# A click predictor's early groups: the recurrence's state as the stationary operand of the first layer

## The chip, the cores and the metric

The kernel runs on one core of one Trainium2 chip. The metric is the device time of one execution in microseconds (us); lower is better. The core has TensorE (PE: matrix products from SBUF into PSUM, each with a weight load of its stationary operand, PEld), VectorE (DVE), ScalarE (ACT), GpSimd (POOL) and SyncE (SP), each with an instruction queue of its own that runs in order. Data come and go by DMA, which SP, POOL and ACT issue.

## The reference

For 1024 users (B) with a history of 100 items (T) of 128 features, all in fp32:

```python
_, gru_seq = scan(gru_step, h0, swapaxes(item_historical_embedding, 0, 1))
keys = swapaxes(gru_seq, 0, 1)
feat = concatenate([keys, q, keys - q, q * keys], axis=-1)      # q: the item, for each step
score = mlp(feat, 80 -> 40 -> 1, relu);  score = where(mask == 1, score, -inf)
attn = softmax(score, axis=1)
pooled = einsum('bt,btd->bd', attn, keys);  att_seq = pooled.T[:T]

def augru_step(h, (x_t, a_t)):                   # second recurrence, over the keys
    r = sigmoid([h, x_t] @ Wr.T + br);  u = a_t[:, None] * sigmoid([h, x_t] @ Wu.T + bu)
    h_hat = tanh([h * r, x_t] @ Wh.T + bh)
    return (1 - u) * h + u * h_hat
attention_feature = the state of step sequential_length - 1 of each user
comb = concatenate([user, item, hist_sum, item * hist_sum, attention_feature], axis=1)   # 640
scores = mlp(comb, 640 -> 200 -> 80 -> 1, sigmoid)               # the predictor; one number a user
```

A user's second recurrence is needed only up to the user's own length.

## The kernel before

Activations lie with features on the 128 partitions and users along the free axis, so a layer is a matmul whose stationary operand is a block of weights. The users are two halves (`NH` = 2) of `HB` = 512.

The first phase (`gru_phase`, up to about 1400 us) runs the first recurrence, the attention network, the softmax and the pooled sums, and computes for each user the part of the predictor's first layer that needs no recurrence, 200 sums per user (`features`), stored as rows in `part_d`. It also ranks the users by length. The change doesn't touch it.

The second phase (`augru_phase`) runs the second recurrence with the users sorted by falling length and dealt to the two halves in turn, so that a step t works on the first `widths[t]` users of each half alone: 512 at t = 0, 428 at t = 18, 70 at t = 88, 32 at the end. There are three copies of the phase, for three sets of widths, of which a count of the lengths chooses one; the data here take the set named `WIDTHS[0]`. The order on every queue is the order in which the program issues (a manual schedule).

`half_step(t, i)` issues, for one half: on TensorE the closing matmul of the other half's candidate (`ph<-r`, line 1131), then this half's `pr` and `pu` from the state `h_all`, then the three opening matmuls of the next half-step from the keys (line 1127); on ScalarE a tanh (line 1139) and two sigmoids (1151, 1152); on VectorE the product with tanh (1155), `r` (1157), the other half's new state `h_all` (1159), `pu` times the attention (1165), `rest` (1168) and then a transpose of keys for two steps ahead (1117). TensorE needs `r` for the next half-step's first matmul and `h_all` for its second. From `one` on (t = 88, 70 users or fewer in a half) `whole_step(t)` takes both halves at once.

Gathers of the keys' rows (`load_row`, lines 187 and 188) run on GpSimd's queue, each behind a one-column copy of `rest`, which paces them.

`predict(g)` is the predictor for a group of 64 users of each half (`PR` = 64, 128 users together). It is a generator: each `yield` is a stop, and the main loop advances the oldest job by one stop per half-step (in whole steps twice per step), from the ninth half-step after the group's last user has ended. Groups 7 to 1 so end within the recurrence, at steps from t = 18 (group 7) to t = 93 (group 1); group 0 (`last`) runs behind the recurrence. In order, a job gathers its rows of `part_d` into `part` (128 users x 200, line 1279); forms the first layer's sums `p0` (two chunks of `MC` = 100 features x 128 users) by transposing `part` onto PSUM with a matmul against the identity (`of_part`, line 1286) and adding the state's product (`of_state`, line 1291: weights stationary, 64 columns of the state moving, once per half); applies the sigmoid (1326); and goes through the second layer (1332, 1337), the third (1340, 1343) and a scatter of the 128 results to `early_d` (line 1345, issued on GpSimd's queue by `rows_of`, line 1271). At the end `earlier_results` loads all early results into `all_y` (line 1381), and the last group adds its own by four matmuls `po` (1349) and a VectorE sum (1357) ahead of the store.

Early jobs take their PSUM tiles from `pa`, a pool of one bank: a job's next tile waits until the last one is read.

Of the kernel before, what the change touches and what calls it, by code (L numbers as in the profile page):

```python
# [9 lines left out]
F32 = mybir.dt.float32  # L10
# [9 lines left out]
P = 128  # L20
B = 1024
T = 100
HB = 512
NH = B // HB
# [7 lines left out]
M0, M1 = 200, 80  # L32
MC = 100
# [44 lines left out]
PR = P // NH  # L78
# [5 lines left out]
def kernel(ctx: ExitStack, tc: tile.TileContext, a: dict, out: bass.AP):  # L84
# [26 lines left out]
    nc = tc.nc  # L111
# [24 lines left out]
    ident = const.tile([P, P], F32, name="ident")  # L136
# [6 lines left out]
    h_all = const.tile([P, NH, HB], F32, name="h_all")  # L143
    h3 = [h_all[:, i, :] for i in range(NH)]
# [15 lines left out]
    rows = {}  # L160
# [828 lines left out]
    def augru_phase(pools, widths, alive):  # L989
# [6 lines left out]
        sp = pools.enter_context(tc.tile_pool(name="sp3", bufs=2))  # L996
# [3 lines left out]
        one = min((t for t in range(T) if widths[t] <= ONE), default=T)  # L1000
# [12 lines left out]
        def bank(name, n=None):  # L1013

            if n is None:
                n = ring.pop(0)
                ring.append(n)
            return ps[n].tile([P, HB], F32, tag="g", name=name)
# [240 lines left out]
        def predict(g, last=False):  # L1259


            m0, m1 = later["m0"], later["m1"]
            n = M0 // MC
            tag = "last" if last else "a"

            def of_pool(name):
                return bank(name) if last else pa.tile([P, HB], F32, tag="a", name=name)


            def rows_of(out_ap, in_ap, o, i):  # L1270
                nc.gpsimd.indirect_dma_start(
                    out=out_ap,
                    out_offset=o and bass.IndirectOffsetOnAxis(ap=idx_p[:, g : g + 1], axis=0),
                    in_=in_ap,
                    in_offset=i and bass.IndirectOffsetOnAxis(ap=idx_p[:, g : g + 1], axis=0),
                )

            part = sp.tile([P, M0], F32, tag=f"part_{tag}", name="part3")
            rows_of(part, part_d, None, True)
            yield  # L1280
            f0 = sp.tile([MC, n, P], F32, name="f0")
            p0 = [of_pool("p0") for _ in range(n if last else 1)]
            p0 = [p0[j if last else 0][:MC, ts(0 if last else j, P)] for j in range(n)]

            def of_part(j):
                nc.tensor.matmul(  # L1286
                    p0[j], lhsT=part[:, ts(j, MC)], rhs=ident, start=True, stop=False
                )

            def of_state(j, i):  # L1290
                nc.tensor.matmul(  # L1291
                    p0[j][:, ts(i, PR)],
                    lhsT=m0[:, 4, ts(j, MC)],
                    rhs=h3[i][:, ts(g, PR)],
                    start=False,
                    stop=i == NH - 1,
                )

            if last and one < T:
                for j in range(n):  # L1300
                    of_part(j)
                yield
                for j in range(n):
                    nc.tensor.matmul(
                        p0[j].rearrange("p (i r) -> p i r", i=NH),
                        lhsT=m0[:, 4, ts(j, MC)],
                        rhs=h_all[:, :, ts(g, PR)],
                        start=False,
                        stop=True,
                    )  # L1310
                yield
            elif last:
                for j in range(n):
                    of_part(j)
                for i in range(NH):
                    for j in range(n):
                        of_state(j, i)
                    yield
            else:
                for j in range(n):  # L1320
                    of_part(j)
                    for i in range(NH):
                        of_state(j, i)
                yield
            for j in range(n):
                nc.scalar.activation(
                    f0[:, j, :], p0[j], AF.Sigmoid, bias=later["c0"][:, j : j + 1]
                )
            yield
            p1 = of_pool("p1")[:M1, :P]  # L1330
            for j in range(n):
                nc.tensor.matmul(  # L1332
                    p1, lhsT=m1[:, j, :], rhs=f0[:, j, :], start=(j == 0), stop=(j == n - 1)
                )
            yield
            f1 = sp.tile([M1, P], F32, name="f1")
            nc.scalar.activation(f1, p1, AF.Sigmoid, bias=later["c1"])
            yield
            p2 = of_pool("p2")[:, 0:1]
            nc.tensor.matmul(p2, lhsT=f1, rhs=later["m2"], start=True, stop=True)  # L1340
            yield
            y = sp.tile([P, 1], F32, name="y")
            nc.scalar.activation(y, p2, AF.Sigmoid, bias=later["c2"])
            if not last:
                rows_of(early_d, y, True, None)
                return
            p = of_pool("po")[:, :BQ]
            for q in range(P // R):
                nc.tensor.matmul(
                    p[ts(q, R), :],  # L1350
                    lhsT=y.to_broadcast([P, R]),
                    rhs=later["places"][q // 2][:, ts(q % 2, BQ)],
                    start=True,
                    stop=True,
                )
            all_y = later["all_y"]
            nc.vector.tensor_add(all_y, p, all_y)
            nc.sync.dma_start(
                out=out.rearrange("(q c) -> q c", c=BQ),
                in_=all_y.rearrange("(q r) c -> q r c", r=R)[:, 0, :],  # L1360
            )
# [65 lines left out]
        for t in range(1, T):  # L1427
# [23 lines left out]
            for g in range(1, HB // PR):  # L1451
                if left <= g * PR < alive[t]:
                    jobs.append([0, predict(g)])
                    if left:
                        next(jobs[-1][1])
            if t == T - G:
                final = predict(0, last=True)
                next(final)
# [98 lines left out]
```

## Time and profile before

| | us |
|---|---|
| median of 3 timed runs | 2017.4 |
| lowest, highest | 2016.58, 2022.05 |
| the profiled execution | 2009.0 |
| its span, first to last instruction | 2007.1 |
| TensorE busy in the span | 1983.7 |
| VectorE busy | 1671.7 |
| GpSimd busy | 1274.2 |
| ScalarE busy | 934.8 |

The profile is one execution; times within it count from the start of its span. A row of a group or of the timeline names line, engine, operation, the tiles written and read, and the shape; in timeline rows of TensorE the shape is first the stationary operand (128*100: 128 rows, 100 columns), then the moving one, and "x2" joins two records that follow each other. An fp32 matmul leaves two records of about equal length. Matmuls overlap, so the sum of their durations is more than the time that they take; the distance between starts is the better measure. In a row of stretches, behind the stretch and its length, stand the busy us (and instructions) of PE, PEld, DVE, ACT and POOL, then the granted share of TensorE's clock, the DMA engines' share and GB/s.

### The profile page before, as it was taken

The numbers are of one execution on the slowest core, as the hardware profiler recorded it, in microseconds if no ns is written. First come the engines' busy times: TensorE is split into PE (matmuls) and PEld (weight loads), VectorE is DVE, ScalarE is ACT, GpSimd is POOL, SyncE is SP. The second block draws the span as 40 slices with busy tenths as digits, with TensorE's granted clock in tenths as the row PEclk, the third lists the DMA queues.
The fourth block names the chain that finished last, engine by engine and source line by source line (L and its number), as shares of the span: only waits on it lengthen the run. The fifth ranks groups of instructions, "written<-read, shape, count | busy, mean of one in ns | idle before, by whom it ended". The sixth has DMA issues, their size and how long they took to land. (4 is left out here: it accounts for less than half of the span.)

```text
span 2007.1 us, 41031 instructions
## 1 busy us (share of the span) xinstructions
PE 1983.7 (99%) x15380; PEld 994.6 (50%) x15380; DVE 1671.7 (83%) x3010; ACT 934.8 (47%) x1672; POOL 1274.2 (63%) x1325
## 2 busy tenths in 40 slices
PE   9999999999999999999999999998899999999998
PEld 2334444444444444444444444434444556678997
DVE  7878999887978888888878798998577777888985
ACT  4444454454544454544444454554343444444553
POOL 0233939669796959496896868898774353445331
PEclk9999999999999999999999999999999999999998
DMA  4443333333334434333333333333443343333331
GB/s 125 98 118 92 107 99 106 91 83 106 115 106 109 121 103 125 115 104 102 103 105 106 107 92 107 108 91 94 123 132 99 94 112 95 93 101 99 84 79 32
DMA packets 242075, 204.85 MB, mean 102 GB/s; under 512 B 59506, under 2 KB 204890, under 8 KB 241866
## 3 DMA queue, kind: packets, MB, share of 16 engines
q1 hardware_dynamic: 227514, 169.37, 30.2%
q0 software_dynamic: 12480, 32.04, 5.8%
q8 instruction: 123, 2.02, 0.4%
q10 hardware_dynamic: 1872, 0.72, 0.1%
q14 instruction: 86, 0.70, 0.1%
HBM read 146.01 MB, written 54.41 MB: 100 GB/s over the span
## 5 line engine op out<-in xcount | busy, mean ns | idle before, releaser
L534 PE MATMUL ps<-x,wih 128*32 128x512 f32 x4800 | 616.3, 593 | 0.0
L534 PE MATMUL ps<-hn,whh 128*32 128x512 f32 x4752 | 610.7, 592 | 1.4 <-ACT hn L582 1.4
L534 PEld LDWEIGHTS ps<-x,wih 128*32 128x32 f32 x4800 | 216.1, 110 | 302.0 <-issue 298.7
L534 PEld LDWEIGHTS ps<-hn,whh 128*32 128x32 f32 x4752 | 214.3, 110 | 298.9 <-issue 295.3
L519 POOL TENSOR_TENSOR xm<-x,m 128x512 f32<-128x512 f32 x200 | 234.9, 1174 | 143.2 <-DMA m<-mask_d 142.9
L546 ACT ACTIVATE r<-ps,brz 128x512 f32<-128x512 f32 x200 | 137.7, 689 | 386.3 <-PE ps L534 386.1
L520 POOL TENSOR_TENSOR hist<-hist,xm 128x512 f32<-128x512 f32 x200 | 257.9, 1290 | 15.7
L188 POOL DMA_INDIRECT rows<-keys_d,idx_k x218 | 211.5, 970 | 80.7 <-POOL rows L187 72.5
L637 POOL TENSOR_TENSOR pooled<-pooled,kw 128x512 f32<-128x512 f32 x191 | 245.0, 1283 | 15.0
L636 POOL TENSOR_TENSOR kw<-kt,e 128x512 f32<-128x512 f32 x191 | 206.2, 1080 | 69.7 <-DVE e L809 69.6
L565 ACT ACTIVATE ps<-ps,bih 128x512 f32<-128x512 f32 x200 | 132.4, 662 | 229.4 <-DVE ps L564 229.4
L700 PE MATMUL pm<-hn,wk 128*32 128x512 f32 x1200 | 221.8, 592 | 0.0
L700 PE MATMUL pm<-kq,wkq 128*32 128x512 f32 x1200 | 221.7, 592 | 0.0
L1139 ACT ACTIVATE c<-ph,bh 128x510 f32<-128x510 f32 (+57 forms) x174 | 88.3, 507 | 261.1 <-PE ph L1131 261.0
L554 DVE SCALAR_TENSOR_TENSOR u<-ps,bhh,r 128x512 f32<-128x512 f32 x198 | 147.5, 745 | 71.3 <-PE ps L534 68.6
L700 PE MATMUL pm<-mv,w 128*32 128x512 f32 (+1 forms) x808 | 195.4, 592 | 0.6 <-DVE e L790 0.6
L569 DVE TENSOR_TENSOR d<-hn,ps 128x512 f32<-128x512 f32 x198 | 136.1, 687 | 35.9 <-ACT ps L565 35.7
L564 DVE TENSOR_TENSOR ps<-ps,u 128x512 f32<-128x512 f32 x200 | 140.0, 700 | 25.9 <-remote 4.5
L582 ACT COPY hn<-ps 128x512 f32<-128x512 f32 x200 | 116.6, 583 | 93.5 <-DVE kq L576 91.8
L570 DVE TENSOR_TENSOR d<-ps,d 128x512 f32<-128x512 f32 x200 | 138.4, 692 | 26.0 <-ACT ps L566 11.6
L187 POOL COPY rows<-rest 128x1 f32<-128x1 f32 x202 | 38.4, 190 | 175.4 <-DVE rest L1168 170.0
L571 DVE TENSOR_TENSOR ps<-ps,d 128x512 f32<-128x512 f32 x200 | 139.9, 700 | 6.8
(224 smaller groups left out, 3111.8 us busy)
## 6 DMA issues: line engine op xcount, KB each, us to landing
x<-in_hist_x SPq DMA_DIRECT2D x210, 256.0 KB
keys_d<-kt SPq DMA_DIRECT2D x48, 1024.0 KB
m<-mask_d SPq DMA_DIRECT2D x200, 128.0 KB
rows<-keys_d,idx_k POOLq DMA_INDIRECT x218, 3.0
s_b<-mv SPq DMA_DIRECT2D x200, 8.0 KB
keys_d<-kt SPq DMA_DIRECT2D x32, 64.0 KB
mask_i<-in_mask SPq DMA_DIRECT2D x8, 200.0 KB
part_d<-part SPq DMA_DIRECT2D x2, 400.0 KB
```

The costliest lines, as they stand in the source:

```text
L188: nc.gpsimd.indirect_dma_start(out=r[:, at, :], out_offset=None, in_=keys_d[q], in_offset=bass.IndirectOffsetOnAxis(ap=idx_k[:, k, i : i + ...
L519: nc.gpsimd.tensor_mul(d, x, m)
L520: nc.gpsimd.tensor_add(acc, acc, d)
L534: nc.tensor.matmul(p[ts(q, R), :], lhsT=w[:, g, ts(q, R)], rhs=v, start=(j == 0), stop=(j == len(parts) - 1),)
L546: nc.scalar.activation(r, pr, AF.Sigmoid, bias=brz[:, 0:1])
L554: nc.vector.scalar_tensor_tensor(out=u, in0=ph, scalar=bhh[:, 2:3], in1=r, op0=ALU.add, op1=ALU.mult,)
L564: nc.vector.tensor_add(pi, pi, u)
L570: nc.vector.tensor_mul(d, pz, d)
L571: nc.vector.tensor_add(pi, pi, d)
L636: eng.tensor_mul(d, k, w)
L637: eng.tensor_add(acc, acc, d)
L700: nc.tensor.matmul(p[i][s, :], lhsT=w[:, s], rhs=v, start=start, stop=stop)
```

## The change

For the early groups alone (not `last`) the first layer is turned round. ScalarE copies the group's state, 64 columns of either half, into one tile `state` of 128x128. TensorE takes that tile as the stationary operand and the 128x200 weights as the moving one, which gives rows: 128 users x 200 features in PSUM. VectorE adds these to `part` in place. TensorE then transposes the two chunks of 100 features of `part` into `p0`, from where the job goes on as before. Between these there are stops of their own: copy, matmul, sum, transposes, so that a job has ten stops to go through where it had seven. The last group's two ways of before (`one < T` or not) become one, which for these widths issues what it issued before.

```diff
             f0 = sp.tile([MC, n, P], F32, name="f0")
-            p0 = [of_pool("p0") for _ in range(n if last else 1)]
-            p0 = [p0[j if last else 0][:MC, ts(0 if last else j, P)] for j in range(n)]
-
-            def of_part(j):
-                nc.tensor.matmul(
-                    p0[j], lhsT=part[:, ts(j, MC)], rhs=ident, start=True, stop=False
-                )
-
-            def of_state(j, i):
-                nc.tensor.matmul(
-                    p0[j][:, ts(i, PR)],
-                    lhsT=m0[:, 4, ts(j, MC)],
-                    rhs=h3[i][:, ts(g, PR)],
-                    start=False,
-                    stop=i == NH - 1,
-                )
-
-            if last and one < T:
+            if last:
+                p0 = [of_pool("p0")[:MC, :P] for _ in range(n)]
                 for j in range(n):
-                    of_part(j)
+                    nc.tensor.matmul(
+                        p0[j], lhsT=part[:, ts(j, MC)], rhs=ident, start=True, stop=False
+                    )
                 yield
...
+            else:
+                state = sp.tile([P, NH, PR], F32, name="state3")
+                nc.scalar.copy(state, h_all[:, :, ts(g, PR)])
                 yield
-            elif last:
+                p = of_pool("rows")[:, :M0]
+                nc.tensor.matmul(
+                    p,
+                    lhsT=state.rearrange("p i r -> p (i r)"),
+                    rhs=m0[:, 4, :],
+                    start=True,
+                    stop=True,
+                )
+                yield
+                nc.vector.tensor_add(part, p, part)
+                yield
+                p = of_pool("p0")
+                p0 = [p[:MC, ts(j, P)] for j in range(n)]
                 for j in range(n):
-                    of_part(j)
-                for i in range(NH):
-                    for j in range(n):
-                        of_state(j, i)
-                    yield
-            else:
-                for j in range(n):
-                    of_part(j)
-                    for i in range(NH):
-                        of_state(j, i)
-                yield
+                    nc.tensor.transpose(p0[j], part[:, ts(j, MC)], ident)
+            yield
             for j in range(n):
                 nc.scalar.activation(
                     f0[:, j, :], p0[j], AF.Sigmoid, bias=later["c0"][:, j : j + 1]
```

## The prediction

> **What bounds the kernel now.** I read the page first (busy time, clock, chain), then the waits and the busy time by stretch for the second recurrence, and last the timeline around one predictor job. The page's first part, and TensorE's clock in 40 slices:
>
> ```profile
> PE 1983.7 (99%) x15380; PEld 994.6 (50%) x15380; DVE 1671.7 (83%) x3010; ACT 934.8 (47%) x1672; POOL 1274.2 (63%) x1325
> ...
> PEclk9999999999999999999999999999999999999998
> ```
>
> TensorE (PE) is busy almost throughout, at full clock until the last slice. The change touches only the seven early predictor jobs, which lie between 1594 and 1990 us. The longest waits of that part (who waits for whom: total us, times, longest):
>
> ```profile
> ACT c L1139 <- PE ph L1131: 261.0, 173, 3.4
> ...
> DVE pu L1155 <- ACT c L1139: 71.7, 113, 1.9
> ```
>
> ScalarE (ACT) waits for TensorE in every half-step, and VectorE (DVE) for ScalarE's tanh in 113 of 173; asked for TensorE's own waits from 1590 to 1966 us, the trace has none. So there TensorE's instructions, one after another, are the time. The timeline of TensorE at the first job (start, us, line, tiles, count):
>
> ```profile
> 1594.08 0.88 PE L1127 MATMUL pu<-k,wu 128*128 128x428 f32 x2
> 1594.80 0.38 PE L1286 MATMUL p<-ident,part 128*100 128x128 f32 x2
> 1595.02 0.48 PE L1291 MATMUL p<-h_all,m 128*100 128x64 f32 x4
> 1595.34 0.41 PE L1286 MATMUL p<-ident,part 128*100 128x128 f32 x2
> 1595.59 0.48 PE L1291 MATMUL p<-h_all,m 128*100 128x64 f32 x4
> 1595.91 0.94 PE L1131 MATMUL ph<-r,wh 128*128 128x428 f32 x2
> ```
>
> Matmuls overlap, so I cost by start-to-start distances. An fp32 matmul is two records (two passes), a transpose one. From 1594.80 to 1595.91 the first layer's six matmuls hold TensorE for 1.11 us; the same block starts at 1700.01, 1787.86, 1904.97, 1947.25 and 1983.07, and takes 1.11 us each time (1.12 the last). The 64-column passes go at 0.08 us each.
>
> **The change, part by part.** Seven jobs (groups 7 to 1). Six lie in half-steps; group 1 lies in the steps that take both halves at once, where TensorE waits at times, so it is costed apart. The last group's path (`last`) keeps its matmuls and its place.
>
> Removed, per job: the block of 1.11 us.
>
> Added on TensorE, per job: one fp32 matmul of 200 columns (state stationary, 128x128), and one half-step pair later two transposes of 100 features.
>
> ```profile
> 1886.12 0.50 PE L1131 MATMUL ph<-r,wh 128*128 128x198 f32 x2
> 1886.46 0.50 PE L1131 MATMUL pr<-h_all,wr 128*128 128x198 f32 x2
> ...
> 1429.51 0.60 PE L1076 MATMUL pw<-ident,att_r 128*32 128x128 f32 x4
> 1429.94 1.43 PE L1053 MATMUL spare<-ident,att_r 128*128 128x128 f32 x8
> ```
>
> The gate matmul at 198 columns has a distance of 0.34 us, which I take for the 200 columns (ends 0.32, the 192-column row, and 0.39, that plus the 0.05 us by which the first matmul after a small block is longer: 0.77 at 1595.91 against 0.72). Four transposes onto 128 columns take 1429.94 - 1429.51 = 0.43 us, so two take 0.215. Their lower end is 0.17 (two 80 ns passes), their upper end 0.47, as if they ran in two passes like line 1286 now (0.22 and 0.25). I take 0.215, since line 1076 is the same instruction. Per job 0.34 + 0.215 = 0.555, saving 1.11 - 0.555 = 0.555 us; six jobs save 3.3 us.
>
> A rule speaks against this. The Trainium skill (TensorE: Matmul & The Clock Gate, Part 4: PE-mode transpose) gives about 275 ns for a transpose in a kernel's context and says the full clock doesn't engage for it. The rows at line 1076 show a duration of 272 ns too, but four of them start within 0.43 us, so the page's figure is latency here. By it as a cost two transposes would be 0.55 us (an estimate from that page), each job would save 0.22 and six 1.3 us.
>
> Added on ScalarE: a copy of 128x128 per job. The nearest row is the copy of 128x200 from PSUM, 308 to 330 ns, so at most 0.33 us. It is issued after a half-step's two sigmoids. In wide half-steps ScalarE then waits up to 3.4 us for the next `ph`; in the narrowest (group 2) its idle time there is 0.30 to 0.93 us (1951.99 to 1954.95). The matmul that needs the copy comes a half-step later (1.3 to 4.3 us). Cost nothing; without that cover, 0.33 per job.
>
> Added on VectorE: the sum of 128x200 from PSUM and SBUF. The nearest row, `r<-h_all,pr` at 128x198, has 0.36 us. It stands behind a half-step's key transpose and ahead of the next `pu<-pu,c`, so `r`, `h_all` and the next transposes of keys are queued behind it. Where no block has just delayed TensorE, that instruction waits for tanh for 0.7 us at group 7 (1619), 0.5 at 6 (1706) and 0.3 at 5 (1799), which hides the sum, all or nearly. At groups 4 to 2 that wait is near nothing:
>
> ```profile
> 1908.53 0.37 DVE L1117 STREAM_TRANSPOSE k<-rows 128x192 f32<-128x192 f32 x1
> ...
> 1908.82 0.33 DVE L1155 TENSOR_TENSOR pu<-pu,c 128x172 f32<-128x172 f32 x1
> 1909.06 0.33 DVE L1157 TENSOR_TENSOR r<-h_all,pr 128x168 f32<-128x168 f32 x1
> ```
>
> There `r` and `h_all` come up to 0.36 us later. The margin of `r` at group 3 is 0.20 us (ended 1907.67, `ph` started 1907.87), of `h_all` 0.24. But the sum delays exactly the half-step whose `r` and `h_all` TensorE needs only behind the two new transposes, which are 0.215 us more: 0.20 + 0.215 covers 0.36. I take 0; the upper end is 0.36 in each of the three narrow jobs, 1.1 us.
>
> A new wait: the transposes wait for the sum. They stand a half-step after it. At group 3 VectorE's key transpose ends 1.03 us into the half-step, the sum would end at 1.4, and TensorE arrives at 1.72; at group 2 about 1.15 against 1.35. Zero, by 0.2 to 0.3 us.
>
> Moved: three more stops per job, so sigmoids, second layer and the result's store come one and a half steps later, and the store by line 1271 goes past three to five row gathers on GpSimd's queue. Those gathers are paced by `rest` of the same half-step anyway; the store waits for a `y` issued before that `rest`. Cost 0. Ends: no gain, as no gather bounds TensorE now, and at most the 4.64 us that GpSimd once waited for `y`, which delays gathers with a landing of 3.1 us but about two steps of lead.
>
> Group 1's store now comes two steps later, near 1994.5 instead of 1990.07. The load of `all_y` waits for it (before: 2.2 us behind the store), so it starts near 1996.8. With the longest landing of the early results' transfers, 3.5 us, it is there by 2000.3; VectorE needs it at 2003.9. Hidden, by 3.6 us. The last group's gather of `part` is no longer behind that store and comes earlier, also hidden.
>
> Group 1 itself: its block lengthened its step (start to start of line 1197's `pr`) from a trend of 2.37 to 3.36 us, 0.99. Now the 200-column matmul waits for a copy that starts when tanh ends (1982.79) and costs about 0.37; the transposes stand directly ahead of `pr<-c` and wait for a sum that stands directly behind the product `c` (0.25 + 0.36 us), so they cost about 0.54 in the next step. The two sigmoids of the first layer no longer stand ahead of the gate's, worth about 0.03. Saved: 0.99 - 0.91 + 0.03 = 0.1 us.
>
> **Sum.** 3.3 + 0.1 = 3.4 us off the profiled execution, 2009.0 to 2005.6 us. (Its span is 2007.1; 1.9 us lie around it and stay.) That execution is 8.4 us under the median of the timed runs, 2017.4, so the forecast is 2017.4 - 3.4 = 2014.0 us. With all upper ends the gain is 6 x (1.11 - 0.39 - 0.47) - 1.1 = 0.4 us; with all lower ends and group 1 free of charge 6 x (1.11 - 0.32 - 0.17) + 0.99 = 4.7 us.
>
> **Rivals.** First, the clock of the tail. TensorE's stretches at the end (stretch, its length, busy us per engine, granted clock):
>
> ```profile
> 1994.00:1995.00 1.00, 0.97 (x9) 0.84 (x8) 0.35 (x2) 0.49 (x2) 0.00 (x0) 1.00 0.24 85
> 1995.00:1996.00 1.00, 1.00 (x8) 0.98 (x8) 0.53 (x3) 0.31 (x1) 0.00 (x0) 0.91 0.07 25
> 1996.00:1997.00 1.00, 1.00 (x6) 0.95 (x5) 0.23 (x1) 0.19 (x1) 0.00 (x0) 0.50 0.00 0
> ```
>
> The clock halves near 1995.8 and stays so. From there matmuls take longer: about 0.3 us in the last steps, 0.6 each for lines 1286 and 1304, 0.5 each for line 1332 and `po`, 0.1 for line 1340: 2.6 in all. Group 1's second and third layer now run two steps later, and so fill TensorE more just before. If the clock held to the end, the time would be 2014.0 - 2.6 = 2011.4. If it fell 3.5 us sooner, two more steps would be slow by 0.4 each: 2014.8. Against it: nothing else in those steps changes, and the job's block is gone from them.
>
> The Trainium skill (same page, Part 1: The HAM clock gate) says the clock falls after an idle window of about 3.4 us that runs free of the kernel. No such idle stretch stands before 1995.8, so by the rule alone the fall would not be explained; it gives no other time.
>
> Second, the change doesn't shorten the path: from group 4 on VectorE has hardly a wait, and at group 2 `pr<-h_all` starts 0.31 us behind `ph` where 0.22 is the weight loads' pace. If the chain through tanh and `h_all` sets the pace at groups 4 to 2, what TensorE saves there becomes waiting: only groups 7 to 5 gain, 1.7 us, and with the sum's 0.36 in three jobs 0.6: 2016.8. Against it: removing a block that ran after `r` and `h_all` were ready moves `ph` forward, since `r` was ended 0.2 us before the block began.
>
> Third, slower: the transposes wait for VectorE's sum in every job, with TensorE's whole queue behind them. It decides from 3.4 / 7 = 0.5 us per job on, and passes +0.3% at (3.4 + 6.1) / 7 = 1.4. A full half-step late, 2 us on average, it would be 2014.0 + 14 = 2028. Against it: the margins above.
>
> **How the numbers follow.** Within 0.3% is 6.05 us here, about what a measurement of this kernel can tell from no change: three runs spread over 5.5 us. My case 0.62, the clock holding 0.15, no shorter path 0.13, slower 0.10. My case and the second rival lie within 0.3% except where runs scatter (2016.6 to 2022.1, and 2009.0 when profiled); the clock's case sits on the edge. Faster takes half of that case and a fifth of mine, 0.21; slower 0.08; within 0.71. The range goes down to 2008, the clock's 2011.4 less 3.4 for scatter, and up to 2020, the second rival's 2016.8 plus 3.2.
>
> **What would show it.** In the changed profile: one matmul of 128x200 in two records per job, 0.34 us to the next start; two single-record transposes, 0.21 together; no idle time of TensorE ahead of them up to group 2; the copy at 0.3 us and the sum at 0.36; the stretch from 1590 to 1966 shorter by 3.3 us. I am wrong if TensorE waits for VectorE there, if the transposes take two records, or if the clock falls at another width of the last steps.

## The result and the profile after

| | before | after |
|---|---|---|
| median (21 runs each), us | 2019.82 | 2013.24 |
| lowest to highest, us | 2016.58 to 2022.05 | 2009.9 to 2016.94 |
| the profiled execution, us | 2009.0 | 2014.8 |
| its span, us | 2007.1 | 2013.0 |

The ratio is 0.9971, with a 95% interval of 0.9965 to 0.9977: 5.9 us faster (4.6 to 7.1), just under the 0.3% (6.05 us) that the prediction named. Gains in us here and below are this ratio times the median of before; the two medians alone differ by 6.6 us. The forecast was 3.4 us faster, from 2017.4 to 2014.0.

The two profiled executions say the opposite of the medians: the one of before is 7.6 us under the lowest of its 21 timed runs. So they can't be compared by their ends, and the work below goes stretch by stretch. Busy time and TensorE's clock, from the page of after:

```profile
PE 1986.5 (99%) x15324; PEld 992.8 (49%) x15324; DVE 1672.2 (83%) x3017; ACT 935.5 (46%) x1679; POOL 1277.1 (63%) x1325
...
PEclk9999999999999999999999999999899999999998
```

TensorE still fills 99% of the span, with 56 records fewer. The 8 within the clock's row is the slice from 1409 to 1459 us, where the clock is at half up to 1416.3 us and again for 3.4 us from 1436.8. The first job in after, on TensorE's timeline, twice: the new matmul, and behind it, a step later, the transposes.

```profile
1604.64 0.88 PE L1127 MATMUL pu<-k,wu 128*128 128x424 f32 x2
1605.35 0.50 PE L1302 MATMUL rows<-m,state 128*128 128x200 f32 x2
1605.69 0.88 PE L1131 MATMUL ph<-r,wh 128*128 128x428 f32 x2
...
1613.50 0.86 PE L1127 MATMUL pu<-k,wu 128*128 128x418 f32 x2
1614.20 0.38 PE L1315 MATMUL p<-ident,part 128*100 128x128 f32 x2
1614.42 0.88 PE L1131 MATMUL ph<-r,wh 128*128 128x424 f32 x2
```

From 1605.35 to 1605.69 are 0.34 us, from 1614.20 to 1614.42 are 0.22: 0.56 us where the old block held TensorE for 1.11. In the stretch of group 7's job (between the first `pr<-k` of 434 and of 388 columns) the profile before has 76.85 us and the one after 76.24; for group 6 (388 to 332) it is 82.22 and 81.62, for group 5 (300 to 270) 36.77 and 36.16. Each job is 0.6 us shorter: 0.55 by the block, and 0.05 because the matmul behind it no longer follows a small block (0.72 us where it was 0.77).

All instructions of the new lines in after (operation, tiles, count: lowest, median and longest ns, first and last start), and who waited for VectorE's sum (us, times):

```profile
L1302 PE MATMUL rows<-m,state x14: 332/333/407, 1605.3 to 1988.7; 128*128 128x200 f32 x14
```
```profile
L1315 PE MATMUL p<-ident,part x14: 272/273/316, 1614.2 to 1991.5; 128*100 128x128 f32 x14
```
```profile
L1310 DVE TENSOR_TENSOR part<-rows,part x7: 325/328/354, 1610.6 to 1990.9; 128x200 f32<-128x200 f32 x7
...
  PEld p L1315: 0.3, 1
  PE p L1315: 0.2, 1
```
```profile
L1299 ACT COPY state<-h_all x7: 287/287/288, 1599.7 to 1988.1; 128x128 f32<-128x128 f32 x7
```

Seven matmuls leave 14 records (two passes), 14 transposes leave 14. One of seven pairs of transposes waited for the sum, 0.2 us (the 0.3 us of PEld is its weight load), that of group 1 (at 1991). TensorE's only wait from 1590 to 1966 us:

```profile
PE pu L1127 <- ACT c L1139: 0.4, 1, 0.4
```

That one wait isn't one that the change makes: TensorE waits for ScalarE's tanh of the recurrence. The profile before had no wait at all there. The experiments lead back to it.

### The profile page after: what moved, and what is told of

Same layout as the page of the kernel before. It is cut to its first block, busy times and chain, and to the rows that moved or that the text cites. A ratio compares the mean times of both kernels' runs of the same rounds, so it can differ in the third digit from the quotient of the medians.

```text
span 2013.0 us, 40935 instructions
## 1 busy us (share of the span) xinstructions
PE 1986.5 (99%) x15324; PEld 992.8 (49%) x15324; DVE 1672.2 (83%) x3017; ACT 935.5 (46%) x1679; POOL 1277.1 (63%) x1325
## 4 chain that ended last, share of the span: by engine, by line
PE 95%; DVE 3%; issue 1%; ACT 1%; ACTq 0%; DVEq 0%
PE ps L534 49%; PE pm L700 17%; PE pr L1131 4%; PE ph L1131 4%; PE pu L1131 4%; PE pr L1127 4%; PE ph L1127 4%; PE pu L1127 4%; PE pr L1204 0%; PE ph L1204 0%; PE p L1324 0%; DVE pu L1155 0%; PE pu L1030 0%; PE pd L243 0%; DVE ps L564 0%
## 5 line engine op out<-in xcount | busy, mean ns | idle before, releaser
L534 PE MATMUL ps<-x,wih 128*32 128x512 f32 x4800 | 775.9, 593 | 0.0
L534 PE MATMUL ps<-hn,whh 128*32 128x512 f32 x4752 | 769.6, 592 | 1.4 <-ACT hn L582 1.4
L534 PEld LDWEIGHTS ps<-x,wih 128*32 128x32 f32 x4800 | 259.0, 110 | 302.0 <-issue 299.1
L534 PEld LDWEIGHTS ps<-hn,whh 128*32 128x32 f32 x4752 | 257.0, 110 | 298.7 <-issue 294.6
L700 PE MATMUL pm<-hn,wk 128*32 128x512 f32 x1200 | 266.4, 592 | 0.1
L700 PE MATMUL pm<-kq,wkq 128*32 128x512 f32 x1200 | 265.8, 592 | 0.0
```

The lines of the kernel that those rows point to most:

```text
L534: nc.tensor.matmul(p[ts(q, R), :], lhsT=w[:, g, ts(q, R)], rhs=v, start=(j == 0), stop=(j == len(parts) - 1),)
L700: nc.tensor.matmul(p[i][s, :], lhsT=w[:, s], rhs=v, start=start, stop=stop)
```

## The experiments

Three sets, each run on one chip together with runs of the kernel before: the first four experiments on a first chip, the next four on a second, the last four on a third. The question was why the gain is 5.9 us and not 3.4. Theory 1: TensorE's own work is the path, and the block's cost is as predicted. Its rivals put the rest on VectorE's chain, on the place of the job's later parts, or on the tail. "Recurrence" below is the time from the first `pr<-k` of 510 columns (about 1417 us) to the first `pr<-c` of 64 columns (about 1990 us) in the profiled execution; the tail is what comes behind it, up to the start of TensorE's last group of matmuls (`po`).

**Only the stops.** The kernel before, with its block three stops later:

```diff
             else:
+                yield
+                yield
+                yield
                 for j in range(n):
                     of_part(j)
```

> The kernel before with the three further stops of the changed one and nothing else: the old first layer of six matmuls stands where the changed kernel has its transposes, and every later part of a job comes one and a half steps later. My theory (TensorE's instructions are the time, and where in the recurrence a job's later parts stand costs nothing): no change, within 1.5 us of before. Rival (the gain beyond the 3.4 us of TensorE's work comes from the later place, by the clock in the tail or by group 1's steps): 2 to 3 us faster than before.

Measured: 2018.33 us against 2021.45, ratio 0.999 (0.9981 to 0.9999), 2.0 us faster (0.2 to 3.8). That lies in the rival's range (2 to 3) and outside theory 1's 1.5, though the interval holds both. So the later place may be worth about 2 us on this chip.

**The changed kernel, started sooner.** So that sigmoids, second layer and store stand where they stood before:

```diff
-                    if n == 0 and job[0] > 2 * G and next(job[1], job) is job:
+                    if n == 0 and job[0] > 2 * G - 3 and next(job[1], job) is job:
```

> The changed kernel with every early job started three half-steps sooner, so that its sigmoids, second and third layer and store stand where they stood before the change. My theory: the same as the changed kernel, within 1.5 us, about 5.9 us faster than before. Rival (the later place gave part of the gain): 2 to 3 us slower than the changed kernel, about 3.4 us faster than before.

Measured: 2014.88 us, ratio 0.9965 (0.9951 to 0.9979), 7.1 us faster (4.2 to 9.9). Not less than the change itself. The rival's 3.4 lies outside the interval, so the later place alone doesn't give the rest of the gain; a part of up to 1.7 us (5.9 - 4.2) the interval leaves open.

**The transposes in two passes.** As matmuls against the identity:

```diff
-                    nc.tensor.transpose(p0[j], part[:, ts(j, MC)], ident)
+                    nc.tensor.matmul(
+                        p0[j], lhsT=part[:, ts(j, MC)], rhs=ident, start=True, stop=True
+                    )
```

> The changed kernel with its two transposes per job made as matmuls against the identity, two passes each. My theory: two passes cost 0.22 + 0.25 us where the transposes cost 0.22 in the trace, so each job loses 0.25 us and the gain shrinks by 1.7 us, to about 4.2 us faster than before. Rival (each microsecond of TensorE's work taken from a job is worth 1.7 us in the timed runs, since the whole gain was 5.9 us for 3.4 us of work): it shrinks by 3 us, to about 2.9 us faster.

Measured: 2015.86 us, ratio 0.9969 (0.9957 to 0.9982), 6.3 us faster (3.6 to 8.7). The rival's 2.9 lies outside the interval. The timed difference to the change is too small for these runs, but the trace has it:

```profile
1612.88 0.60 PE L1315 MATMUL p<-ident,part 128*100 128x128 f32 x4
1613.32 0.88 PE L1131 MATMUL ph<-r,wh 128*128 128x424 f32 x2
```

Four records and 0.44 us where the transposes have two and 0.22. Group 7's stretch becomes 76.46 us against 76.24. So a transpose is half the price of the matmul that does the same, as I had counted it.

**The old block twice.** The kernel before, with the early first layer computed two times:

```diff
-                for j in range(n):
-                    of_part(j)
-                    for i in range(NH):
-                        of_state(j, i)
+                for _ in range(2):
+                    for j in range(n):
+                        of_part(j)
+                        for i in range(NH):
+                            of_state(j, i)
```

> The kernel before with the early groups' first layer computed twice over, in the same place (the second time overwrites the first). My theory: seven more blocks of 1.11 us, one by one on TensorE: 7.0 to 7.8 us slower than before. Rival (a microsecond of a job's TensorE work is worth 1.7 us): 12 to 13 us slower. Second rival (TensorE has hidden slack at groups 4 to 2): under 6 us slower.

Measured: 2028.48 us, ratio 1.0035 (1.0021 to 1.0048), 7.1 us slower (4.2 to 9.7): seven blocks of 1.0 us. That excludes the first rival (12 to 13); the second (under 6) only the trace excludes. Group 7's stretch has 77.99 us against 76.85, and set against the kernels of before on the third chip the traces grow by the same 1.14 us at each of the six jobs in half-steps, groups 4 to 2 included. So 1.1 us of TensorE's time in a job is 1.1 us of the kernel's time; this is the strongest support for the sum's base.

**Both kernels once more, unedited, on another chip.**

> The kernel before against itself: how far two sets of runs of one kernel differ, and a second profile of it, since the first is 8 to 11 us under its own timed runs. Theory 1 (the 2.5 us of gain beyond the forecast are scatter): a ratio within 1 +- 0.001. Theory 2 (the kernel before has late starts of single instructions in most runs, which its first profile happens to lack, and which the change makes rarer): ratio 1 as well, but a profile of about 2018 us with several microseconds of late tanh or sums between 1420 and 1980 us.

> The changed kernel once more, on the same chip as the other three: a second measurement of the gain. Theory 1 (scatter): 3 to 5 us faster than before, so that both measurements together come nearer the 3.4 us forecast. Theory 2 (something beyond TensorE's work is gained): 5.5 to 6.5 us again.

Measured: before 2019.69 us, ratio 0.9999 (0.999 to 1.0008); after 2012.9 us, ratio 0.9971 (0.9961 to 0.9981). The 5.9 us came out again. And this time the profiled execution of before, 2019.3 us, is like its timed runs, with the late starts that theory 2 expected.

**No sum.** The changed kernel without `nc.vector.tensor_add(part, p, part)`, so that the early users' results lack the state's share:

> The changed kernel without VectorE's sum: the product with the state is computed and left unread, and the transposes take the part alone, so the early users' results lack the state's share. My theory (the sum lies beside TensorE's work): the same as the changed kernel, within 1 us. Rival (the sum holds TensorE up at groups 4 to 1): 1.0 to 1.5 us faster than the changed kernel.

Measured: 2012.31 us, ratio 0.9965 (0.9951 to 0.9978), 7.1 us faster (4.4 to 9.9), which is not to be told from the change's 5.9, nor does the interval exclude the rival's 1.0 to 1.5 us. The traces decide: the stretches of groups 7, 6 and 5 have the same length to 0.01 us with the sum and without it (76.24 for group 7), and at the jobs of groups 4 to 2 they differ only where the late starts lie that are treated below. VectorE's sum is hidden, as predicted.

**The part alone.** The kernel before with its block cut to the two transposes of `part`, with no product of the state:

```diff
                 for j in range(n):
-                    of_part(j)
-                    for i in range(NH):
-                        of_state(j, i)
+                    nc.tensor.transpose(p0[j], part[:, ts(j, MC)], ident)
                 yield
```

> The kernel before, with its seven stops, whose early first layer is cut to the two transposes of the part: no product with the state at all. TensorE's block falls from 1.11 to 0.22 us, with 0.05 us at the following matmul. Theory 1 (TensorE's work alone is gained): 0.94 us a job, 6.0 to 6.6 us faster than before. Theory 2 (shedding the block gains 2.5 us beyond the work, wherever it comes from): 8.5 to 9 us faster.

Measured: 2011.09 us, ratio 0.9965 (0.9955 to 0.9976), 7.1 us faster (4.9 to 9.1). Theory 1 said 6.0 to 6.6, theory 2 8.5 to 9: the ratio's value is nearer to the first, the difference of the two medians (8.6 us) to the second, and the interval excludes neither. In the trace group 7's stretch is 75.90 us, 0.95 less than before, as theory 1 has it.

**What the repeated profile of before shows.** From 1420 us on it has late starts of ScalarE that the first profile doesn't have. ScalarE's timeline around the half-step of 152 columns (start, us, line, and in brackets the idle time before it):

```profile
1925.11 0.35 ACT L1151 ACTIVATE pr<-pr,br 128x152 f32<-128x152 f32 x1
1926.26 0.36 ACT L1152 ACTIVATE pu<-pu,bu 128x152 f32<-128x152 f32 x1 [0.80 <-PE pu L1127]
1928.46 0.39 ACT L1139 ACTIVATE c<-ph,bh 128x152 f32<-128x152 f32 x1 [1.84 <-PE ph L1127]
```

And TensorE at the same place:

```profile
1925.91 0.48 PE L1131 MATMUL ph<-r,wh 128*128 128x152 f32 x2
...
1926.99 0.41 PE L1127 MATMUL ph<-k,wh 128*128 128x146 f32 x2
1928.90 0.52 PE L1127 MATMUL pu<-k,wu 128*128 128x146 f32 x2 [1.50 <-ACT c L1139]
```

The tanh at 1928.46 needs the `ph` that ended at 1925.91 + 0.48 = 1926.39, and ScalarE has been free since 1926.62. It starts 1.8 us late, and the releaser that the profile names, a matmul of the next half-step, is none. TensorE then idles for 1.50 us. At the start of the recurrence the same kernel's ScalarE is late with a copy by much more: it starts 5.1 us behind the end of the matmul that it copies. ScalarE's waits from 1425 to 1990 us (who waits for whom: total us, times, longest):

```profile
ACT c L1139 <- PE pu L1127: 17.5, 14, 2.5
...
ACT at L1070 <- remote: 7.2, 1, 7.2
```

That copy delays TensorE by 2.3 us, and behind the idle time TensorE's clock is granted at 0.53 and 0.61 (1434 to 1438 us).

The changed kernel on the same chip is late at the same tanh, but by 0.5 us (the `ph` that it needs ended at 1921.52 + 0.50 us; TensorE's row, then ScalarE's):

```profile
1921.52 0.50 PE L1131 MATMUL ph<-r,wh 128*128 128x152 f32 x2
```
```profile
1922.53 0.39 ACT L1139 ACTIVATE c<-ph,bh 128x152 f32<-128x152 f32 x1 [1.13 <-PE pu L1131]
```

I had a suspect: GpSimd's scatter of early results (line 1271) among its row gathers. In the nine profiles of this kind all 68 tanh and sigmoids that start more than 0.45 us late stand 1.5 to 3.2 us behind the start of a gather or scatter, where of the others 53 to 55% do. And this half-step goes with the place of the job's later parts, the store among them: from the first `pr<-k` of 152 columns to that of 142 are 8.42 us here, 8.41, 8.45 and 8.15 in the three others with these at the old place (block twice, part alone, sooner start), but 6.98 to 7.07 in the five with them at the later one, among which is the kernel before with the stops alone. In the profiles without late starts it is 6.38 to 6.56. The third set tests the suspect.

**The store alone later.** The kernel before with three stops ahead of the early store:

```diff
             if not last:
+                yield
+                yield
+                yield
                 rows_of(early_d, y, True, None)
```

> The kernel before, with three more stops ahead of the early results' store only (the last statement of a job), so that it stands behind the following row gathers on GpSimd's queue, as in the changed kernel; first layer, sigmoids and second layer stay where they were. Theory 1: the place of the store among the row gathers is what costs the kernel before some 2 us by late starts of ScalarE around the half-step of width 152: 1.5 to 2.5 us faster than before, and the stretch from width 198 to 80 shorter by about 2 us (81.6 to 79.6). Theory 2: the place of the sigmoids and the second layer, or nothing in particular, makes that difference: no change from before (within 1 us).

**Without the early stores,** for before and for after (the early users' results are missing): the line `rows_of(early_d, y, True, None)` is taken out.

> The kernel before without the early results' stores; it leaves those results out of the output. Theory 1: ScalarE's late starts come with those stores: 3 to 4 us faster than before. Theory 2: the row gathers or something else than the stores cause them: within 1 us of before.

> The changed kernel without the early results' stores; it leaves those results out of the output. Theory 1: the stores cost less at their later place, so 1 to 2 us are gained on the changed kernel (7 to 8 faster than before), less than the same edit gains on the kernel before. Theory 2: within 1 us of the changed kernel (5 to 7 faster than before).

**The sooner start again,** the same edit as the second experiment:

> The changed kernel with its early jobs started three stops sooner, so that sigmoids, second layer and store stand where they did before (a repeat of the kernel that measured 7.1 us faster, interval 4.2 to 9.9). Theory 1: with the store at its old place only the removed work is left, 3.6 us faster than before (2.5 to 4.7). Theory 2: the store's place is not what made the rest: 6 to 7 us faster again.

Measured on the third chip, where the kernel before has a median of 2008.42 us (28 runs, 2004.74 to 2011.58), against 2021.45 and 2019.72 on the first two:

| | us | ratio, interval | recurrence, us | tail, us |
|---|---|---|---|---|
| store later | 2008.29 | 1.0001 (0.9991 to 1.001) | 571.76 | 12.19 |
| before, no store | 2008.36 | 0.9997 (0.9988 to 1.0006) | 571.75 | 16.32 |
| after, no store | 2004.6 | 0.9977 (0.9967 to 0.9987) | 567.75 | 14.37 |
| after, sooner | 2004.83 | 0.9976 (0.9966 to 0.9987) | 567.31 | 15.80 |

Neither the store's place nor the store itself makes a difference here. The sooner start is now worth 3.6 us by the medians and 4.8 us by the ratio (2.6 to 6.8), where it was 7.1 (4.2 to 9.9) on the first chip. But on this chip the late starts are missing too. ScalarE's waits from 1425 to 1990 us in the kernel with the later store:

```profile
ACT c L1139 <- PE ph L1131: 260.8, 173, 3.4
...
ACT at L1070 <- PE spare L1053: 2.3, 2, 2.1
```

173 times the tanh is released by its own `ph`, as in the first profile of before (261.0, 173); in the repeated one 143 times. The recurrence in the profiles, by chip:

| | late starts | before | after | after, sooner |
|---|---|---|---|---|
| third chip | none | 571.8 (both edits) | 567.8 (without store) | 567.3 |
| first profile of before | none | 572.2 | | |
| the others' profiles | many | 582.6 | 574.5, 574.8 | 575.5 |

Where ScalarE starts on time the change is worth 4.0 us of recurrence, or 4.4 with the sooner start. Where it doesn't, it is about 8.0 us: there the recurrence of before is 10.9 us longer than without late starts, and that of the changed kernel 6.7 to 7.0. (In these profiles its tail is longer by 0.6 to 1.7 us, 13.0 and 14.2 against 12.4, which brings the 8.0 nearer to the measured 5.9.) So by these profiles, one execution each, the gain beyond the work's is a part of those late starts that the changed kernel doesn't meet or bears better. The timed runs alone don't show it: on the third chip the change without stores gains 4.6 us (2.6 to 6.6), and that interval holds 5.9 too.

The profiles show two parts of it. One is the half-step of 152 columns above, 1.4 us shorter in the changed kernel than in the one before, as it is with the stops alone, which gained 2.0 us (0.2 to 3.8). The other is TensorE's clock, which is at half for 3.4 us at times: twice within the recurrence in the repeated profile of before (from 1434.1 and from 1980.3 us), once in each of the two profiles of the changed kernel (from 1436.8 and from 1970.4 us). Over all nine it is once or twice in the four of the kernel before and its edits, and none to two times in the five of the changed one and its edits, so this part may be chance.

Which of the moved parts matters stays open. The store as the cause is neither shown nor refuted, since the chip on which it was tried had none of the late starts; and the sooner start, with its store at the old place and 8.2 us of them in its profile of the first chip, gained as much there (7.1 us, from an interval that reaches down to 4.2) as the change does. No set ran that kernel beside the unedited changed one, so the runs don't tell the two apart.

## Why the prediction was right, and where it was not

- **TensorE's order is the path:** right. The doubled block costs its own 1.14 us in the stretch of its job, and 7.1 us in all; and groups 4 to 2, where the second rival saw no gain, save 1.96 us together on the third chip. So that rival, a path through VectorE that the block's removal does not shorten, falls; so does the third, as TensorE waits for the sum in one job only.
- **The terms on TensorE:** right. The matmul has 0.34 us between starts (predicted 0.34), the two transposes 0.22 (0.215). The 0.05 us that I used for the upper end was there on the good side, at the matmul behind the block, and I did not count it: six jobs are 3.8 us on the third chip (three of 0.61, three of together 1.96), not 3.3.
- **The page's figure as a cost:** refuted for throughput. The Trainium skill (TensorE: Matmul & The Clock Gate, Part 4: PE-mode transpose) gives about 275 ns for a transpose; the records here have a median of 273 ns (272 to 316), but two take 0.22 us of TensorE's time. With that figure as the cost six jobs would have saved 1.3 us (an estimate from that page), where they saved 3.8.
- **Copy and sum at nothing:** right. No matmul waited for the copy (287 ns; one weight load did, for 0.2 us), and without the sum the jobs' stretches are no shorter. The transposes' wait was zero in six jobs and 0.2 us in group 1, where it was predicted.
- **Group 1, 0.1 us:** 0.2 on the third chip (its stretch of whole steps is 20.95 us against 21.17). The wait came where it was predicted: the pair of transposes at 1980.91 waits 0.18 us and takes 0.27 to the next start, 0.45 together where I had counted 0.54. With the sooner start that stretch is 20.25, and the pair no longer waits. From that kernel's timeline and then from that of the changed one without stores:

```profile
1978.01 0.38 PE L1315 MATMUL p<-ident,part 128*100 128x128 f32 x2
1978.22 0.42 PE L1204 MATMUL pr<-c,wr 128*128 128x80 f32 x2
```
```profile
1980.91 0.43 PE L1315 MATMUL p<-ident,part 128*100 128x128 f32 x2 [0.18 <-DVE part L1310]
1981.18 0.34 PE L1204 MATMUL pr<-c,wr 128*128 128x68 f32 x2
```

- **The results' load hidden:** right. In after the last sum, into `all_y`, waits for the last matmul `po` and not for the load:

```profile
DVE all_y L1349 <- PE po L1341: 4.9, 1, 4.9
```

- **The tail's clock as a rival:** its mechanism is there, but the clock's fall moves without the change too. The two edits of the kernel before on the third chip reach the tail at 1989.1 and 1988.9 us and differ by 4.1 us in it; the clock falls at 1999.7 in one and at 1990.1 in the other, and behind the fall matmuls take longer: the four records of line 1286 have 1.12 us where they have 0.63 ahead of it (stretch, length, busy us per engine, clock). The later store:

```profile
1990.00:1991.00 1.00, 0.97 (x9) 0.81 (x8) 0.68 (x5) 0.38 (x2) 0.78 (x1) 1.00 0.00 0
...
1999.00:2000.00 1.00, 0.73 (x4) 0.43 (x4) 0.00 (x0) 0.44 (x3) 0.00 (x0) 0.84 0.00 0
```

Without stores:

```profile
1989.00:1990.00 1.00, 1.00 (x9) 0.89 (x8) 0.36 (x4) 0.75 (x3) 0.00 (x0) 1.00 0.00 0
1990.00:1991.00 1.00, 0.97 (x6) 0.95 (x5) 0.55 (x3) 0.29 (x1) 0.00 (x0) 0.57 0.00 0
```

I had priced a clock that holds to the end at 2.6 us and one that falls 3.5 us sooner at 0.8. The range is wider: tails of the profiles run from 12.2 to 16.3 us.
- **The step that failed:** "That execution is 8.4 us under the median of the timed runs, 2017.4, so the forecast is 2017.4 - 3.4 = 2014.0 us." I carried the difference along as a constant. It was no constant: the profile lacked ScalarE's late starts (10.9 us of the recurrence in the repeated profile, which at 2019.3 us is like the timed runs), and in the profiles the changed kernel loses less to them (6.7 and 7.0 us). So 3.4 us were predicted, the recurrence's work gave 4.0, and 5.9 were measured. The first profile's 2009.0 us also lies within the range of the third chip (2004.74 to 2011.58) and under every run of this kernel on the other two; the record doesn't name its chip, so it may come from one like the third.
- **Luck in the number:** 2014.0 lies 0.8 us from the measured 2013.24 because two errors cancel. The median of the three runs from which I counted, 2017.4, is 2.4 us under that of 21 runs (2019.82), and the gain was put 2.5 us too low (3.2 by the two medians).
- **Two small slips:** the 173 and 113 waits that I showed for the jobs' part are those of the whole second recurrence (from 1590 to 1966 us there are 139 and 82), and the chances for "faster" add up to 0.20, not 0.21.

## What to carry to other kernels

Where one engine's queue is full, an edit is worth the difference of start-to-start distances, and the same operation done twice is a cheap proof of it. If the profiled execution lies far outside the timed runs, it may lack something that they have, or come from another chip: profile once more before its waits are taken for the kernel's. And compare two traces by stretches between the same two instructions, since the tail alone scattered by 4 us.

## What was not expected of the hardware

- The same kernel takes 2008.4 us on one chip and 2019.7 and 2021.5 on two others, with ranges that don't meet (2004.74 to 2011.58 against 2015.74 or more on the others). In the profiles 10.9 us of it lie in the recurrence, at late starts of ScalarE for which the profile has no releaser, and at two stretches of 3.4 us with TensorE's clock at half. Their cause wasn't found. They aren't scattered at random: all nine profiles that have them have one at a half-step of 152 columns and one at 122, and eight have one at 198.
- All of these late starts of more than 0.45 us came 1.5 to 3.2 us behind the start of an indirect DMA of GpSimd, but on the third chip the same DMAs came with none.
- At the end of the kernel TensorE's clock falls to half, at a place that differs by 9 us between two kernels whose tails do the same; TensorE is busy at 0.97 to 1.00 around the fall in one and at 0.68 to 0.73 in the other. In every trace the granted clock changes only at whole multiples of 3.41 us from its earlier changes (with the later store at 1402.35, 1412.59 and 1999.68 us, 3 and 172 steps apart). On the third chip runs of before with a mean clock of 0.997 took 2004.7 to 2006.9 us and those with 0.993 took 2010.4 to 2011.6.
